# Binding statistics, Newton steps and list pieces behind the y copies on VectorE, and spreading attention's steps up to tile 129

## The chip, the cores and the metric

The kernel runs on one core of a Trainium2 chip. The metric is the device time of one execution in microseconds (us), as the median of several executions. The engines are TensorE (PE, with its weight loads as PEld), VectorE (DVE), ScalarE (ACT), GpSimd (POOL) and SyncE (SP, which here only issues transfers). Transfers that read or write through a list of row numbers (gathers and scatters) are issued by POOL.

## The reference, cut to what matters

8192 tokens of 256 values in 8 sequences of 1024. A layernorm, causal linear attention with 16 heads of 16, and a mixture of 8 experts of which each token uses two; the output is the input plus both.

```python
xn = (x - mean) / sqrt(var + 1e-5)
# attention
q, k = elu(xn @ Wq.T) + 1, elu(xn @ Wk.T) + 1
v = xn @ Wv.T
kv_cumsum = cumsum(k * v over the tokens of a sequence); k_cumsum = cumsum(k)
out = (q . kv_cumsum) / clip(q . k_cumsum, 1e-6, None)
attn = out @ Wo.T
# experts, H = 256, I = 512, E = 8
w, e = top_k(xn @ Wr + br, 2); w = softmax(w)
ffn = sum over the two of w * ((silu(xn @ W1[e]) * (xn @ W3[e])) @ W2[e])
result = x + attn + ffn
```

## The kernel before, in words

**Blocks and attention.** The tokens are worked in 16 blocks of 512 (NBLK), each of 4 chunks of 128 (NCH). Attention is a generator (`block_steps`, L1106) that yields 8 steps for each block and one more at the end, 129 in all (LAST). Below, step b.s is step s of block b. Steps 0 to 2 project q, k and v. Step 3 computes the denominators (den L980; VectorE's over and reciprocal), the scores of chunk 0, and `attend` for the last chunk of the block before. Steps 4 to 7 each take one chunk: `scores` (s_ps L1011, masked by VectorE into s_sb L1018), `carry` (the state of the earlier chunks times q, into o_ps L1030), `weigh` (the scores times v L1048, the new state kv, VectorE's oT L1065 and kv), and `attend` for the chunk before: a_ps L1091 on PE, a copy to at on ACT L1096, and for every second chunk a transfer by POOL (L1099) that adds two chunks of at, one half of a block, to the output in memory. "at(b14 h1)" would be the second half of block 14.

**Expert tiles.** The experts' work is cut into 132 tiles (NM) of 128 rows of one expert. Tiles 0 to 24 (N1 = 25) take tokens of the first four blocks (FB = 4) and are ready at the start; the others take the rest, and their lists of tokens are made while the first tiles run. Some spare tiles follow under a condition. `ffn_step(j)` (L1429) issues: the gathers of later tiles (`ffn_load`, POOL, L1297 and L1302), the weights of tile j + 2 (SP), gate and up for tile j (gu_ps L1391 on PE, silu on ACT L1399, the product hT on VectorE L1402), the second product of tile j - 1 (y_ps L1410 on PE, and its scaled copy y on VectorE, L1417, "the y copy"), and the store of an older tile, a transfer by POOL that adds the rows of y to the output (L1421). What POOL adds to the output, from attention and from tiles, goes in the order in which it is issued.

**Work beside the tiles.** `tile_step(j)` (L1481) is called for each tile. Beside `ffn_step` and attention's steps it holds:

- in tiles 0 to 11, the preparation of block t = 4 + j: the transposes of the normalised block (`turn`, tp L357), its router logits (lg_ps, lg_t), the statistics of a block to come (`stats`, L298: for each of four chunks a bn_stats and a bn_aggr), and for every second block the inverse deviations of two blocks (`deviations`, L307: 17 small VectorE operations, with four Newton iterations for the inverse square root). `normalise(t + 1)` (ACT) needs the deviations, and `turn(t + 1)` in the next tile needs the normalised block;
- in tiles 4, 8 and 12 ("counting" tiles) a part of `route` (L417): VectorE ranks the experts of four blocks, PE counts them (cnt_ps L483), VectorE works the counts into places;
- in tiles 14 to 21, and once in tile 22 (READ = 22), pieces of `second_batch` (L741), a generator that makes the list of the other tiles. `piece(place)` takes its next piece at five places of each tile: ahead of attention's step (0), behind it (1), between the two halves of gate and up (2), behind them (3) and at the tile's end (4). A piece makes two one-hot tables on VectorE (at_place L606 and held L619) and five products on ACT (parts, L624 and L626); the next call multiplies them on PE (held_ps L771), and every fourth of them sums into all_held on VectorE.

**Order.** PE's order is the order of the program text (the tile loop runs under a manual schedule for PE). The other engines are ordered by a scheduler, unless the program binds an instruction behind another: `in_order(...)`, and `tc.issue_after(x)`, under which everything issued goes behind instruction x. Before the change, the routing work of a tile and the statistics and deviations are under `issue_after(last_masked)`, that is behind the latest mask or reciprocal of attention (`last_token` in the first three tiles).

**Buffers of PE's results.** The pool ps_y has two banks, used in turn by y_ps, a_ps, den, lg_ps, lg_t, cnt_ps and held_ps; ps_mm has four, for gu_ps, s_ps and the projections; ps_t has two, for the transposes and o_ps with kv_ps.

**Where attention's steps go.** `attend_upto(upto, put_off=True)` runs steps until `upto` of them are made; most tiles get one step, and where two are due, the second is in some cases left to a later tile or put off behind the gate and up of the same tile. Up to tile 22 the steps are few. From tile 22 on they go by a straight line that reaches the last step at END = NM - 11 = 121: thirteen of these tiles hold two steps, and tiles 122 to 131 none.

Of the kernel before, what the change touches and what calls it, by code (L numbers as in the profile page):

```python
# [51 lines left out]
ALU = mybir.AluOpType  # L52
# [12 lines left out]
def tile_attention_moe(  # L65
# [14 lines left out]
    nc = tc.nc  # L80
# [5 lines left out]
    NCH = TB // P  # L86
    N = B * L
    NBLK = N // TB
# [5 lines left out]
    FB = 4  # L94
# [4 lines left out]
    NM = NF - NR  # L99
# [45 lines left out]
    for t in range(FB):  # L145
        xbs[t] = e_one.tile([P, NCH, H], F32, name=f"xb{t}")
        step = NCH // 2 if t == 0 else NCH
        for c in range(0, NCH, step):
            some = slice(c, c + step)
# [148 lines left out]
    def stats(t, mv):  # L298
        st = f_two.tile([P, NCH, 6], F32, tag="st", name="st")
        for c in range(NCH):  # L300
            nc.vector.bn_stats(st[:, c, :], xbs[t][:, c, :])
            nc.vector.bn_aggr(mv[:, c, :], st[:, c, :])

    def moments_tile(n):
        return f_two.tile([P, n * NCH, 2], F32, tag="mv", name="mv")
# [24 lines left out]
    def normalise(t):  # L330
        xb = xbs.pop(t)
        less, rstd = (tab[:, t * NCH : (t + 1) * NCH, w] for w in (1, 2))
        for c in range(NCH):
            if t < FB and (c % 2 == 0 or t == FB - 1):
                nc.vector.tensor_scalar(
                    xb[:, c, :], xb[:, c, :], rstd[:, c : c + 1], less[:, c : c + 1],
                    ALU.mult, ALU.add,
                )
            else:
                done = nc.scalar.activation(  # L340
                    xb[:, c, :], xb[:, c, :], AF.Identity, bias=less[:, c : c + 1],
                    scale=rstd[:, c : c + 1],
                )
                if t > FB:
                    in_order(done)
        scaled[t] = xb
# [478 lines left out]
    def fetch(t):  # L825
        xnTs[t] = two.tile([P, KC, TB], F32, tag="xnT", name="xnT")
        in_order(
            nc.sync.dma_start(out=xnTs[t].rearrange("p k l -> p (k l)"), in_=xnT_d[t])
        )
# [194 lines left out]
    def carry(t, c):  # L1024

        both_ps = ps_t.tile([P, KC * P + KC * PAIR], F32, tag="t", name="o_ps")
        if t % BLK_PER_SEQ or c:
            o_ps = both_ps[:, 0 : KC * P].rearrange("p (k l) -> p k l", k=KC)
            for hh in range(KC):
                nc.tensor.matmul(  # L1030
                    o_ps[:, hh, :], lhsT=state[0][:, hh, :],
                    rhs=blocks[t][0][:, hh, bass.ts(c, P)],
                    start=(hh == 0), stop=False, skip_group_check=True,
                )
        return both_ps
# [70 lines left out]
    def block_steps(t):  # L1106


        yield from project(t)
        denominators(t)  # L1110
        if t + 1 < NBLK:
            fetch(t + 1)
        waiting = scores(t, 0)
        if behind:
            attend(*behind.pop())
        yield
        done = None
        for c in range(NCH):
            if done:
                attend(*done)  # L1120
            both_ps = carry(t, c)
            coming = scores(t, c + 1) if c + 1 < NCH else None
            oT = weigh(both_ps, *waiting)
            done = t, c, oT
            waiting = coming
            yield
        behind.append(done)
        if t + 1 == NBLK:
            attend(*behind.pop())
            yield  # L1130

    STEPS = 8
    LAST = NBLK * STEPS + 1
# [4 lines left out]
    def attention():  # L1138
        for t in range(NBLK):
            yield from block_steps(t)  # L1140
# [17 lines left out]
    with tc.manual_schedule(engines={EN.DVE, EN.Activation, EN.PE, EN.Pool}):  # L1158
# [85 lines left out]
        mv = moments_tile(1)  # L1244
# [6 lines left out]
    for a in range(4):  # L1251
        some = slice(a * E // 4, (a + 1) * E // 4)
# [35 lines left out]
    ys = {}  # L1288
    entry = {}
# [18 lines left out]
    def ffn_norm(j):  # L1308
        in_order(
            nc.scalar.activation(  # L1310
                xg[j], xg[j], AF.Identity, bias=entry[j][:, 1:2], scale=entry[j][:, 2:3]
            )
        )
# [91 lines left out]
    def ffn_out(j, last=False):  # L1405
        hT = hs.pop(j)
        e = expert_of(j, mybir.EngineType.PE)
        y_ps = ps_y.tile([P, H], F32, tag="y", name="y_ps")
        for i in range(IC):
            done = nc.tensor.matmul(  # L1410
                y_ps, lhsT=hT[:, i, :], rhs=w2_sb[:, bass.ds(e * (IC * H) + i * H, H)],
                start=(i == 0), stop=(i == IC - 1),
            )
            if last:
                in_order(done)
        ys[j] = ffn5.tile([P, H], F32, tag="y", name="y")
        nc.vector.tensor_scalar(ys[j], y_ps, entry.pop(j)[:, 0:1], None, ALU.mult)  # L1417

    def ffn_store(j):
        _, _, _, _, rows, dst_i, i = of_tile(j)  # L1420
# [51 lines left out]
                nc.sync.dma_start(out=wo_sb, in_=woT.rearrange("(k p) o -> p k o", p=P))  # L1472
            )
    LATE = 3
    END = NM - 11
    LISTS = NBLK - FB
    READ = LISTS + 10
    AHEAD = 2 + LISTS // 2 + READ - LISTS
    held = {}

    def tile_step(j):  # L1481
        nonlocal routing
        if j + 1 < TURNED:
            ffn_norm(j + 1)
        if TURNED <= j + 2 < NM:
            ffn_norm(j + 2)
            ffn_halves(j + 2)
        t = FB + j
        turning = 0 < j and t < NBLK
        counting = FB < t <= NBLK and t % ROUND == 0  # L1490

        def piece(place):
            if LISTS + 2 <= j < READ or (j, place) == (READ, 0):
                next(held["lists"])

        def between():
            if turning:
                turn(t)
                if t + 5 < NBLK:
                    load_x(t + 5, nc.scalar)  # L1500
            piece(2)

        def after():
            piece(3)

        def late():
            nonlocal waits
            if waits:
                attend_upto(waits)
                waits = None  # L1510

        def finish():
            if turning:
                held["lgT"] = f_two.tile([P, P], F32, tag="lgT", name="lgT")
                nc.scalar.copy(held["lgT"], logits(t))
            if counting:
                next(routing)
            if t + 1 < NBLK:
                normalise(t + 1)

        if LISTS <= j < LISTS + NBLK - FB:
            rows = slice((t - LISTS) * TB, (t - LISTS + 1) * TB)
            in_order(nc.sync.dma_start(out=out_rows[rows, :], in_=x_rows[rows, :]))
        piece(0)
        if j < LISTS:
            upto = 3 + j // 2
        elif j < READ:
            upto = AHEAD - (READ - j - 1)
        else:
            upto = AHEAD + (LAST - AHEAD) * (j - READ + 1) // (END - READ + 1)  # L1530
        waits = attend_upto(upto, put_off=True)
        if t <= NBLK:
            with tc.issue_after((last_token if j < 3 else last_masked)[0].ins):
                if "lgT" in held:
                    tp = ps_y.tile([P, P], F32, tag="y", name="lg_t")
                    nc.tensor.transpose(tp, held.pop("lgT"), ident)
                    add_logits(t - 1, 1, tp)
                if routing and not counting:
                    for _ in routing:
                        pass  # L1540
                    routing = None
                if counting:
                    routing = route(t - ROUND, t)
                    next(routing)
                of_blocks = [] if j == 0 else [t + 1, t + 2] if j == 1 else [t + 2]
                for a in of_blocks:
                    if a < NBLK:
                        if a % 2 == FB % 2:
                            held["mv"] = moments_tile(2)
                        some = slice(0, NCH) if a % 2 == FB % 2 else slice(NCH, 2 * NCH)  # L1550
                        stats(a, held["mv"][:, some])
                        if a % 2 != FB % 2:
                            deviations(a - 1, 2, held.pop("mv"))
        piece(1)
        ffn_step(j, LATE if N1 < j <= N1 + LATE else 0, between, after, late, finish)
        piece(4)
        if j == LISTS:
            for _ in routing:
                pass
            in_order(  # L1560
                nc.sync.dma_start(
                    out=tab_d[1][1 : 1 + NS * P, :].rearrange("(p i) w -> p (i w)", p=P),
                    in_=tab.rearrange("p i w -> p (i w)"),
                )
            )
            in_order(nc.sync.dma_start(out=tab_d[1][0:1, :], in_=before[0:1, 0:3]))
            held["lists"] = second_batch(taken)
            next(held["lists"])
        if j == N1 + 1:
            copied.append(j)  # L1570
            in_order(nc.sync.dma_start(out=out_rows[0 : FT * P, :], in_=acc_d[:, :]))
# [59 lines left out]
```

## Time and profile before

| quantity | value |
|---|---|
| median of 5 runs | 1278.82 us (1272.17, 1280.89, 1285.35, 1271.82, 1278.82) |
| the profiled execution | 1282.86 us |
| its span, first to last instruction | 1281.2 us |
| mean clock granted to TensorE | 0.982 of full speed |
| busy: PE, DVE, ACT, POOL | 1206.7, 686.2, 588.6, 549.8 us |
| moved by DMA | 252.68 MB, mean 197 GB/s |

The page of the profile shows one execution: busy time of each engine; the span in 40 slices of 32 us, with a digit for the busy tenths of each; the costliest groups of instructions, as line, engine, operation, result and operands, with count, busy time, mean of one, and the idle time of the engine ahead of them with what ended most of it. The timeline shows single instructions or runs of equal ones: start (us from the span's start), duration, engine, line, tiles, and in brackets the idle time ahead and what ended it. The waits list groups of an engine's idle time by the waiting instruction and by what released it: total us, count, longest. Windows give the busy time of each engine within stretches of the span.

### The profile page before, as it was taken

What the parts mean: (1) busy time and instruction counts of PE and PEld (TensorE: products, weight loads), DVE (VectorE), ACT (ScalarE), POOL (GpSimd) and SP (SyncE); (2) the same over time, 40 slices, a digit from 0 to 9 for tenths busy, and PEclk for the clock granted to TensorE, in tenths of its full rate; (3) what the DMA queues carried; (4) which work ended last, traced back from release to release, by engine and by line L of the source; (5) the groups of instructions that cost most, each with busy time, mean ns of one, the idle gap of its engine ahead of it and who ended that gap; (6) DMA issues with size and microseconds to landing.
All of it is one profiled execution on the core that took longest, in us unless ns stands there. A gap on an engine that the chain in (4) does not pass through costs nothing. (4 is left out here: it accounts for less than half of the span.)

```text
span 1281.2 us, 29841 instructions
## 1 busy us (share of the span) xinstructions
PE 1206.7 (94%) x11394; PEld 1056.3 (82%) x11394; DVE 686.2 (54%) x1537; ACT 588.6 (46%) x1098; POOL 549.8 (43%) x474
## 2 busy tenths in 40 slices
PE   8699999899999999999999999999999999999992
PEld 6588887777979888889898989888888888888992
DVE  7676569754444555455554555454535464546320
ACT  5555576592352626262626262626262626262230
POOL 4633343325354544444444444444444444444342
PEclk9899999999999999999999999999999999999996
DMA  9798676558798988988898989898989788978992
GB/s 332 262 276 238 180 220 193 153 162 186 187 224 188 183 212 170 217 168 216 198 198 185 201 183 198 185 201 182 193 193 218 166 215 168 220 164 193 202 234 26
DMA packets 232463, 252.68 MB, mean 197 GB/s; under 512 B 101474, under 2 KB 156386, under 8 KB 232034
## 3 DMA queue, kind: packets, MB, share of 16 engines
q1 hardware_dynamic: 189298, 198.61, 55.0%
q0 software_dynamic: 38272, 43.22, 25.1%
q10 hardware_dynamic: 4752, 8.91, 2.1%
q8 instruction: 94, 1.54, 0.5%
q14 instruction: 47, 0.39, 0.1%
HBM read 187.91 MB, written 44.29 MB: 181 GB/s over the span
## 5 line engine op out<-in xcount | busy, mean ns | idle before, releaser
L1391 PE MATMUL gu_ps<-xgT,w 128*128 128x128 f32 x4224 | 511.3, 279 | 16.7 <-issue 6.1
L1391 PEld LDWEIGHTS gu_ps<-xgT,w 128*128 128x128 f32 x4224 | 495.0, 194 | 35.6 <-issue 17.7
L1421 POOL DMA_INDIRECT out_dram<-y,dst_i x107 | 174.3, 1629 | 273.6 <-DVE y L1417 78.2
L1410 PE MATMUL y_ps<-w_sb,hT 128*128 x1056 | 250.8, 380 | 1.3 <-DVE hT L1402 0.9
L1297 POOL DMA_INDIRECT xg<-in_x_dram,src_i x132 | 135.7, 1028 | 269.4 <-DVE half L1320 155.1
L1399 ACT ACTIVATE hT<-gu_ps 128x512 f32<-128x512 f32 x132 | 79.3, 601 | 315.3 <-PE gu_ps L1391 268.5
L1410 PEld LDWEIGHTS y_ps<-w_sb,hT 128*128 128x128 f32 x1056 | 190.4, 190 | 23.6 <-issue 1.7
L1018 DVE TENSOR_TENSOR s_sb<-s_ps,causal 128x512 f32<-128x512 f32 x256 | 160.2, 680 | 86.3 <-PE s_ps L1011 71.8
L1402 DVE TENSOR_TENSOR hT<-gu_ps,hT 128x512 f32<-128x512 f32 x132 | 90.5, 685 | 67.8 <-PE gu_ps L1391 39.3
L1302 POOL DMA_INDIRECT entry<-tab_d,of_i x107 | 107.7, 1006 | 32.6 <-issue 32.3
L1320 DVE COPY half<-xg 128x512 uint16<-128x512 uint16 x105 | 45.6, 434 | 134.2 <-ACT xg L1310 124.1
L1417 DVE TENSOR_SCALAR y<-y_ps,entry 128x256 f32<-128x256 f32 x132 | 63.6, 482 | 97.0 <-PE y_ps L1410 87.8
L1096 ACT COPY at<-a_ps 128x256 f32<-128x256 f32 x64 | 23.8, 372 | 166.2 <-PE a_ps L1091 166.2
L1310 ACT ACTIVATE xg<-xg,entry 128x256 f32<-128x256 f32 x132 | 78.9, 599 | 7.7 <-DMA entry<-tab_d,of_i 5.3
L1338 ACT COPY xgT<-halfT 128x512 uint16<-128x512 uint16 x105 | 80.1, 763 | 3.3 <-DMA halfT<-half 3.3
L1011 PE MATMUL s_ps<-qm,kT 32*128 32x256 f32 x1024 | 74.8, 403 | 0.0
L1091 PE MATMUL a_ps<-wo_sb,oT 128*128 128x256 f32 x256 | 68.6, 391 | 6.1 <-DVE oT L1065 4.1
L1048 PE MATMUL o_ps<-s_sb,va 128*32 128x128 f32 x2048 | 70.4, 276 | 1.6 <-issue 1.6
L1421 POOL DMA_INDIRECT acc_d<-y,src_i x25 | 43.5, 1741 | 59.8 <-DVE y L1417 25.6
L1048 PEld LDWEIGHTS o_ps<-s_sb,va 128*32 128x32 f32 x2048 | 52.3, 109 | 20.4 <-issue 18.5
L1091 PEld LDWEIGHTS a_ps<-wo_sb,oT 128*128 128x128 f32 x256 | 46.3, 190 | 18.4 <-DVE oT L1065 5.1
L842 PE MATMUL zq<-xnT,wq_sb 128*128 128x512 f32 x128 | 59.0, 603 | 0.0
(236 smaller groups left out, 1399.6 us busy)
## 6 DMA issues: line engine op xcount, KB each, us to landing
w<-in_w_dram SPq DMA_DIRECT2D x264, 512.0 KB
rden<-over SPq DMA_DIRECT2D x128, 64.0 KB
xnT<-xnT_d SPq DMA_DIRECT2D x15, 512.0 KB
out_dram<-at POOLq DMA_DIRECT2D x27, 256.0 KB
out_dram<-in_x_dram SPq DMA_DIRECT2D x12, 512.0 KB
xnT_d<-xnT ACTq DMA_DIRECT2D x11, 512.0 KB
xb<-in_x_dram SPq DMA_DIRECT2D x9, 512.0 KB
w_sb<-in_w_dram SPq DMA_DIRECT2D x4, 1024.0 KB
```

The lines of the kernel that those rows point to most:

```text
L1018: last_masked[0] = nc.vector.tensor_tensor(sm, s_ps[r].rearrange("p k a l -> p (k a) l"), causal_b, ALU.mult)
L1048: nc.tensor.matmul(o_ps[32 * r : 32 * r + 32, hh, :], lhsT=va[:, c, 4 * hh + r, a, :], rhs=s_sb[r][:, 2 * hh + a, :], start=(first and a = ...
L1091: nc.tensor.matmul(a_ps, lhsT=oT[:, hh, :], rhs=wo_sb[:, hh, :], start=(hh == 0), stop=(hh == 1),)
L1297: rows = nc.gpsimd.indirect_dma_start(out=xg[j], out_offset=None, in_=x_rows[:, :], in_offset=bass.IndirectOffsetOnAxis(ap=src_i[:, i : i ...
L1302: nc.gpsimd.indirect_dma_start(out=entry[j], out_offset=None, in_=table[:, :], in_offset=bass.IndirectOffsetOnAxis(ap=num_i[:, i : i + 1], ...
L1310: nc.scalar.activation(xg[j], xg[j], AF.Identity, bias=entry[j][:, 1:2], scale=entry[j][:, 2:3])
L1338: nc.scalar.copy(xgT[j].bitcast(U16).rearrange("p k (l b) -> p b k l", b=2), halves.pop(j).rearrange("p (b k) l -> p b k l", b=2),)
L1391: done = nc.tensor.matmul(ps[:, i, :], lhsT=w13[:, k, bass.ts(i, P)], rhs=xgT[j][:, k, :], start=(k == 0), stop=(k == KC - 1),)
L1399: silu = nc.scalar.activation(hT, gu[0], AF.Silu)
L1402: nc.vector.tensor_tensor(hT, gu[1], hT, ALU.mult)
L1410: done = nc.tensor.matmul(y_ps, lhsT=hT[:, i, :], rhs=w2_sb[:, bass.ds(e * (IC * H) + i * H, H)], start=(i == 0), stop=(i == IC - 1),)
L1421: nc.gpsimd.indirect_dma_start(out=rows[:, :], out_offset=bass.IndirectOffsetOnAxis(ap=dst_i[:, i : i + 1], axis=0), in_=ys.pop(j), in_off ...
```

## The change

Three things are edited.

1. In `block_steps`, a chunk's `carry` is issued ahead of `attend` for the chunk before, on PE, and no longer behind it.
2. `ffn_out` keeps the latest y copy in `held_y`. The list pieces are issued under `issue_after(held_y)`, so that what they issue goes behind the latest y copy on VectorE. The statistics of tile 1 and of the counting tiles, and all deviations, move to `finish()`, which runs behind `ffn_out`, also under `issue_after(held_y)`; the deviations stand there directly ahead of `normalise` in the tile where they are needed, and in tile 1 the statistics of block 6 stay where they were and those of block 7 move. The statistics of the other tiles stay behind the masks.
3. The line along which attention's steps are spread from tile 22 on now ends at tile 129 (NM - 2 is 130, and the 108 tiles from 22 to 129 share the steps) and no longer at 121. Three tiles hold two steps (56, 97 and 129), and tiles 130 and 131 none.

```diff
@@ block_steps
         for c in range(NCH):
+            both_ps = carry(t, c)
             if done:
                 attend(*done)
-            both_ps = carry(t, c)
@@ ffn_out
-        nc.vector.tensor_scalar(ys[j], y_ps, entry.pop(j)[:, 0:1], None, ALU.mult)
+        held_y[0] = nc.vector.tensor_scalar(ys[j], y_ps, entry.pop(j)[:, 0:1], None, ALU.mult)
+
+    held_y = [None]
@@
-    END = NM - 11
...
+    def take_stats(t):
+        second = t % 2 != FB % 2
+        if not second:
+            held["mv"] = moments_tile(2)
+        stats(t, held["mv"][:, second * NCH : (second + 1) * NCH])
@@ piece
-                next(held["lists"])
+                with tc.issue_after(held_y[0].ins):
+                    next(held["lists"])
@@ finish
             if t + 1 < NBLK:
+                if j > 0:
+                    with tc.issue_after(held_y[0].ins):
+                        if t + 2 < NBLK and (counting or j == 1):
+                            take_stats(t + 2)
+                        if t + 2 < NBLK and t % 2 != FB % 2:
+                            deviations(t + 1, 2, held.pop("mv"))
                 normalise(t + 1)
@@ tile_step
-            upto = AHEAD + (LAST - AHEAD) * (j - READ + 1) // (END - READ + 1)
+            upto = min(LAST, AHEAD + (LAST - AHEAD) * (j - READ + 1) // (NM - 2 - READ))
@@ tile_step, under issue_after(last_masked)
-                of_blocks = [] if j == 0 else [t + 1, t + 2] if j == 1 else [t + 2]
-                for a in of_blocks:
-                    if a < NBLK:
-                        if a % 2 == FB % 2:
-                            held["mv"] = moments_tile(2)
-                        some = slice(0, NCH) if a % 2 == FB % 2 else slice(NCH, 2 * NCH)
-                        stats(a, held["mv"][:, some])
-                        if a % 2 != FB % 2:
-                            deviations(a - 1, 2, held.pop("mv"))
+                if t + 2 < NBLK and j > 0 and not counting:
+                    take_stats(t + 1 if j == 1 else t + 2)
```

## The prediction

> **What bounds the kernel now.** I read the page first: busy shares and the slices.
>
> ```profile
> span 1281.2 us, 29841 instructions
> PE 1206.7 (94%) x11394; PEld 1056.3 (82%) x11394; DVE 686.2 (54%) x1537; ACT 588.6 (46%) x1098; POOL 549.8 (43%) x474
> ...
> PE   8699999899999999999999999999999999999992
> ```
>
> TensorE (PE) is busy 94% of the span, so only its 74.5 us of idle time can be won. Next, the windows of 20 us: some 20 us of idle lie before 100, 15 between 100 and 320, 17 between 320 and 1240, and 22.9 after PE's last matmul. The change works on the second and the last. The timeline of the end, whole and for POOL alone, with start and duration:
>
> ```profile
> 1256.31 1.99 PE L1410 MATMUL y_ps<-w_sb,hT 128*128 x8 [0.85 <-DVE hT L1402]
> 1258.34 0.48 DVE L1417 TENSOR_SCALAR y<-y_ps,entry 128x256 f32<-128x256 f32 x1 [2.09 <-PE y_ps L1410]
> ```
>
> ```profile
> 1184.66 1.62 POOL L1421 DMA_INDIRECT out_dram<-y,dst_i  x1 [0.90 <-DVE y L1417]
> ...
> 1190.81 1.32 POOL L1099 DMA_DIRECT2D out_dram<-at  x1 [3.24 <-ACT hT L1399]
> ...
> 1200.19 1.63 POOL L1421 DMA_INDIRECT out_dram<-y,dst_i  x1 [6.68 <-issue]
> ...
> 1264.66 1.55 POOL L1421 DMA_INDIRECT out_dram<-y,dst_i  x1 [2.91 <-issue]
> 1269.27 1.55 POOL L1421 DMA_INDIRECT out_dram<-y,dst_i  x1 [3.05 <-DMA out_dram<-y,dst_i]
> 1273.82 1.55 POOL L1421 DMA_INDIRECT out_dram<-y,dst_i  x1 [3.01 <-issue]
> ```
>
> Each store into the output starts when the one before it has landed. At 1184.66 POOL stores a tile 0.3 us after its y copy; the last y copy ends at 1258.82 and is stored at 1273.82, 15.0 us late. POOL fell behind in the ten tiles without attention (PE spends 5.30 us on each, POOL's stores stand 5.1 to 7.3 us apart there). The third view is the waits of PE between 60 and 320, the fourth the windows behind the longest of them (columns: length, busy time of five engines, granted clock, DMA share, GB/s):
>
> ```profile
> PE cnt_ps L483 <- DVE mv L302: 3.8, 2, 2.0
> PE a_ps L1091 <- DVE oT L1065: 3.6, 2, 2.6
> PE den L980 <- DVE y L1417: 2.0, 2, 1.2
> PE a_ps L1091 <- DVE y L1417: 1.9, 2, 1.0
> ```
>
> ```profile
> 100.60:104.00 3.40, 3.40 (x21) 3.40 (x20) 3.11 (x19) 1.43 (x2) 1.07 (x2) 0.56 0.53 100
> 142.10:145.50 3.40, 3.40 (x18) 3.30 (x17) 2.79 (x18) 1.71 (x2) 1.12 (x2) 0.52 0.43 50
> ```
>
> PE waits for VectorE's (DVE's) counts and y copies, and after each of the two waits for cnt_ps it also runs at half clock for 3.4 us.
>
> **The spreading, on PE.** 111 steps fall on 108 tiles instead of 100: three tiles hold two steps instead of thirteen, and two tiles at the end none instead of ten. No instruction is added. Tiles without attention show no PE idle, and a step's own waits go with it, so PE's end stays: 0, between -3 and +3 (the six waits of gu_ps for ACT's at copy, 4.7 us in all, may lengthen or vanish by some half). Carry ahead of attend swaps 0.61 us and 1.03 us of matmuls: 0, but for one place counted below.
>
> **The spreading, at the end.** Steps 127 and 128 move from tile 121 to tile 129. I lay the end of the new order on the old trace: steps 125 to 128 with their tiles look as at 1174 to 1197, where gu_ps of the last attention tile starts (1196.99). From gu_ps of tile 129 to the last matmul PE took 1239.39 to 1258.30, 18.9 us; so PE would end at 1215.9 on this scale. All gathers are issued by then. POOL's order is store 126, at, store 127, at, then stores 128 to 131. Distances from start to start: store to at 4.65 (1157.84 to 1162.49) or 6.15 (1184.66 to 1190.81); at to store 6.36 (1162.49 to 1168.85) or 9.38 (1190.81 to 1200.19); store to store 4.55 at the end. Store 126 starts at 1184.66. Taking the middle for the first pair, where the weights of the old trace load as well, and the short ones behind, where gathers and then weights have ended: 1184.66 + 5.40 + 7.87 + 4.65 + 6.36 + 4.65 + 4.55 + 4.55 = 1222.7 for store 131; its y is ready at 1216.4. From the last store's start to the end the old trace took 7.4: 1230.1, or 14.2 us after PE instead of 22.9. Gain 8.7. With every short row it is 11.3; with every long row (and 5.38, 1254.82 to 1260.20, for the last three) -0.4.
>
> **Statistics and Newton steps.** The instructions stay, their place on DVE changes. Gains: in the counting tiles the route's chain is no longer cut by statistics, so the waits for cnt_ps go: 1.76 + 2.01 + 0.26, and with them the half clock (gu_ps 3.39 and 2.94 us instead of 1.95: 2.4), and one lg_t wait of 0.59: 7.1. Loss: in tile 1 the y copy can start at 68.8, and behind it now stand, in the new order, the statistics of block 7 and then block 6's Newton steps, mixed with the mask s_sb of tile 2 and with statistics of blocks 8 and 9. From start to start in this stretch a statistics pair takes 0.41, a small step among others 0.1, a mask 0.61: 0.40 for the copy, 1.55 for block 7, 1.95 for over, its reciprocal and the first small steps, 2.85 for four masks with a step each, 3.65 for ten Newton steps, six and a half statistics pairs and lg_all: the deviations are ready at 79.2. ACT then normalises block 6 (2.08), and PE, whose transposes of it ran at 74.74, can go on with gu_ps at 82.0 instead of 75.61: 6.4 lost, and one more half clock, 1.4. Behind it in queue on ACT stand only xg and the copies for the same tile. In tile 4, fifteen Newton steps of 0.20 stand ahead of the first mask, and gu_ps waits for the bank that it frees, then the transposes for ACT: 1.6. Tiles 6, 8 and 10 have attend and carry between (1.6 us more of matmuls), which hide it; without that cover they would cost 1.6 each. Sum 7.1 - 9.4 = -2.3. Bounds: +1.5 (tile 2 costs 5.0 and tile 4 0.6) and -7.8 (the small steps at their whole duration of 0.17, tile 4 2.2, and no clock won back).
>
> The Trainium skill, TensorE: Matmul & The Clock Gate, Part 1, says that the clock halves after at least one idle window of about 3.4 us. The row differs: 0.56 follows a wait of only 1.76. By the page 2.4 of the gain would not be there, and the whole would come to 5.4 instead of 7.8.
>
> **List pieces (tiles 14 to 22).** The y copy now follows hT directly. PE's waits for it at den, at_ps and twice a_ps (1.19, 0.97, 0.97, 0.96: 4.1) go, since held_ps and y hold both y banks there. What is late next is the first piece of each tile, behind the copy: copy, all_held, at_place, held 2.2, then ACT's parts 1.4 behind the at copy: 3.95 after y_ps, while PE needs it after attention's step, at 4.3. Hidden by 0.35. In tile 17 three held in a row stand ahead of the masks, and the last needs parts that ACT finishes late: gu_ps waits 1.4 for its bank, and carry, now first, waits 0.9 for kv; in tile 18 0.4. Sum 4.1 - 2.7 = +1.4; bounds +4.1 and -9.5 (1.7, the third held behind parts at 5.35 plus a mask against 4.85, in eight tiles, 13.6).
>
> **Sum.** 8.7 - 2.3 + 1.4 = 7.8. The profiled execution took 1282.9 (span 1281.2 and 1.7 around it), 4.0 above the median of the five runs; taken off that median, 1278.8, it gives 1271.0.
>
> **Rivals.** Slower: VectorE's pieces become the bound. If in all eight list tiles held stands ahead of the masks as in tile 17, PE loses 1.7 and, through the half clock, 1.4 in each, 24.8; the sum is 8.7 - 2.3 + 4.1 - 24.8 = -14.3: 1293.1. It passes 1% from 2.9 us a tile. For it: DVE was busy 17.84 of 20 us from 200 to 220. Against: in most tiles of the new order a mask comes before the third held.
> The end doesn't clear: at in the queue costs 9.4 twice, POOL stays as late as before, gain 0 there: -0.9, 1279.7. For it: the row at 1190.81. Against: no gathers stand between any more.
> Faster: the short rows hold at the end (11.3), the stall of tile 2 is small (+1.5) and lists win their 4.1: 16.9, 1261.9. For it: unloaded stores stand 4.55 apart. Against: the Newton steps are behind the copy in the order itself.
>
> **How the numbers follow.** Forecast 1271.0: 0.50, own range 1264 to 1277. The end doesn't clear 0.13, slower rival 0.14, faster rival 0.23. 1% is 12.8 us, about what a measurement of this kernel can tell from no change (its five runs span 13.5). A small part of the forecast (0.02) lies below 1266: faster 0.25, same 0.61, slower 0.14. The range, 1261 to 1285, takes in all but the slower rival.
>
> **What would show it.** Right: PE's last matmul 11 to 17 us before the span's end, and stores at the end 4.6 apart; no wait for cnt_ps; one wait of tp (L357) near 76, some 5 to 6 us, on ACT's xb; no wait of a_ps or den for y between 195 and 260. Wrong: a tail of 20 us or more; gu_ps waiting for s_sb in every list tile; PE's busy time at the start as before.

## The result, and the profile after

The changed kernel takes 1282.84 us (median of 37 runs, 1274.41 to 1288.40), the kernel before, over all its runs, 1278.37 us (63 runs). The ratio is 1.0036, with a 95% interval from 1.0025 to 1.0048: by the ratio 4.6 us longer, where 7.8 us shorter were forecast. The profiled execution took 1286.1 us, 3.3 above the median, much as that of before (1282.86, 4.5 above).

From the page of the changed kernel:

```profile
span 1284.4 us, 29801 instructions
PE 1210.7 (94%) x11394; PEld 1051.3 (82%) x11394; DVE 687.6 (54%) x1537; ACT 588.1 (46%) x1098; POOL 550.4 (43%) x474
...
PE   8689998898999999999999999999999999999994
```

The last slice went from 2 tenths to 4, so the tail became shorter; the third, seventh and tenth slice (64 to 96, 193 to 225 and 289 to 321 us) read 8 where 9 stood. The end, from the timeline of all engines (POOL's stores and PE's last matmuls):

```profile
1242.42 1.27 POOL L1099 DMA_DIRECT2D out_dram<-at  x1 [3.35 <-issue]
1250.74 1.64 POOL L1423 DMA_INDIRECT out_dram<-y,dst_i  x1 [7.05 <-issue]
1256.64 1.28 POOL L1099 DMA_DIRECT2D out_dram<-at  x1 [4.26 <-DMA out_dram<-y,dst_i]
1261.94 1.63 POOL L1423 DMA_INDIRECT out_dram<-y,dst_i  x1 [4.02 <-DMA out_dram<-at]
...
1266.49 1.99 PE L1410 MATMUL y_ps<-w_sb,hT 128*128 x8 [0.85 <-DVE hT L1402]
...
1277.15 1.56 POOL L1423 DMA_INDIRECT out_dram<-y,dst_i  x1 [3.03 <-DMA out_dram<-y,dst_i]
```

PE ends at 1268.5 and the span 15.9 us later, instead of 22.9. But PE itself ends 10.2 us later than before (1258.3). The waits of PE between 175 and 336 us, over the list tiles, show most of the reason (total us, times, longest):

```profile
PE held_ps L771 <- ACT parts L626: 7.1, 6, 4.1
PE o_ps L1030 <- DVE kv L1077: 2.2, 1, 2.2
PE o_ps L1030 <- DVE kv L1068: 1.4, 1, 1.4
PE held_ps L771 <- DVE at_place L606: 1.3, 1, 1.3
PE held_ps L771 <- DVE kn L812: 1.2, 1, 1.2
...
PE den L980 <- DVE y L1417: 0.2, 1, 0.2
```

The same view of the kernel before has

```profile
PE held_ps L771 <- ACT parts L626: 1.7, 2, 1.5
```

The waits for y are gone, as the change has it (0.2 instead of 4.1), and the products of the lists now wait for parts that ACT makes (7.1 instead of 1.7).

To see where time goes in kernels whose steps lie in other tiles, I take four marks from PE's timeline: the start of y_ps for tiles 0, 12, 25 and 131. Between tile 12 and 25 lie the list tiles; the steps differ between the kernels only from tile 31 on. The tail runs from the end of the last matmul to the end of the span.

| traced execution | 0 to 12 | 12 to 25 | 25 to 131 | tail |
|---|---|---|---|---|
| before | 120.1 | 146.7 | 922.6 | 22.9 |
| changed | 122.3 | 155.2 | 920.8 | 15.9 |
| difference | +2.2 | +8.5 | -1.8 | -7.0 |

With 1.3 us that the changed kernel's trace was later at the first mark, these add up to 3.2, the difference of the spans. The list tiles cost more than the tail brought. These are single executions, and some of what they show (a half clock behind a wait, the length of the tail) differs between executions of the same code, as the experiments show; 1 to 2 us in one column say little.

### The profile page after: what moved, and what is told of

The parts are those of the page before. It is cut to its first block, busy times and chain, and to the rows that moved or that the text cites. A ratio compares the mean times of both kernels' runs of the same rounds, so it can differ in the third digit from the quotient of the medians.

```text
span 1284.4 us, 29801 instructions
## 1 busy us (share of the span) xinstructions
PE 1210.7 (94%) x11394; PEld 1051.3 (82%) x11394; DVE 687.6 (54%) x1537; ACT 588.1 (46%) x1098; POOL 550.4 (43%) x474
## 4 chain that ended last, share of the span: by engine, by line
PE 84%; DVE 6%; ACT 3%; DMA 3%; issue 2%; another core or an unknown queue 1%; SPq 0%; POOL 0%; POOLq 0%; ACTq 0%; DVEq 0%
PE gu_ps L1391 36%; PE y_ps L1410 17%; PE s_ps L1011 5%; PE o_ps L1048 5%; PE a_ps L1091 4%; PE zkk L863 4%; PE zkv L863 4%; PE zq L842 4%; PE o_ps L1030 2%; PE tp L357 1%; DVE s_sb L1018 1%; PE held_ps L771 1%; PE den L980 1%; PE o_ps L1058 1%
## 5 line engine op out<-in xcount | busy, mean ns | idle before, releaser
L1402 DVE TENSOR_TENSOR hT<-gu_ps,hT 128x512 f32<-128x512 f32 x132 | 90.6, 686 | 79.2 <-PE gu_ps L1391 47.2
L1048 PEld LDWEIGHTS o_ps<-s_sb,va 128*32 128x32 f32 x2048 | 52.8, 111 | 21.6 <-issue 21.5
L1011 PEld LDWEIGHTS s_ps<-qm,kT 32*128 32x128 f32 x1024 | 47.6, 186 | 23.0 <-issue 17.7
L1099 POOL DMA_DIRECT2D out_dram<-at x27 | 36.0, 1332 | 53.8 <-DMA out_dram<-y,dst_i 34.5
```

The source lines that it names most:

```text
L1011: nc.tensor.matmul(s_ps[r][:, hh].rearrange("p a l -> p (a l)"), lhsT=kT[rows, hh, span], rhs=qm[rows, hh, :, span], start=True, stop=True,)
L1048: nc.tensor.matmul(o_ps[32 * r : 32 * r + 32, hh, :], lhsT=va[:, c, 4 * hh + r, a, :], rhs=s_sb[r][:, 2 * hh + a, :], start=(first and a = ...
L1402: nc.vector.tensor_tensor(hT, gu[1], hT, ALU.mult)
```

## The experiments

They ran in four sets, each beside runs of the kernel before. Each set ran on a chip of its own. That kernel took 1275.51 us in the first set and 1247.22, 1247.43 and 1248.41 in the others; so ratios are always against before in the same set, and the marks of the first set are not set against those of the others. The chip of the result above is not on record; its traces look like those of the first set.

### First set: one part at a time

**Spreading alone.** The list pieces, statistics and carry stay as before.

```diff
-            upto = AHEAD + (LAST - AHEAD) * (j - READ + 1) // (END - READ + 1)
+            upto = min(LAST, AHEAD + (LAST - AHEAD) * (j - READ + 1) // (NM - 2 - READ))
```

> Only the third edit: attention's steps spread up to tile 129, the rest as before. Theory A (the tail and the list tiles carry the result): the tail after PE's last matmul shrinks from 22.9 to about 16 us, as in the changed kernel's profile (15.9), and PE's end stays: 1271.5 us, ratio 0.9945. Rival B (the spreading itself costs PE in the middle of the kernel, at the tiles that now hold a step, what it brings at the end): 1278 to 1282 us, with the same short tail but PE's last matmul 7 to 10 us later than before.

**List pieces alone.**

```diff
-                next(held["lists"])
+                with tc.issue_after(held_y[0].ins):
+                    next(held["lists"])
```

> Only the list pieces are bound behind the y copy; carry, statistics and spreading as before. Theory A: the loss of the changed kernel arises in tiles 14 to 22, where PE's lag grew from 3.5 us (tile 12) to 13 us (tile 22): 1286 to 1289 us, ratio 1.007, with PE waiting some 7 us in held_ps for ACT's parts, above all in tiles 20 and 21, which hold projection steps. Rival C (the waits of o_ps for kv, 2.2 and 1.4 us, come with carry ahead of attend, and the pieces alone take away 4.1 us of waits for y): 1275 to 1279 us.

**Statistics and Newton steps alone.** The edits of `finish` and of `tile_step` behind `issue_after(last_masked)`, as in the change.

> Only the statistics and the Newton steps are bound behind the y copy. Theory A: as the step of the prediction has it, a loss of about 2.3 us (tile 2 loses 6, the waits for cnt_ps go): 1280.7 us, ratio 1.002. Rival D (the stall of tiles 2 to 4, where the lag went to 10.2 us, is worth more than what the counting tiles give back): 1284 us or more. Rival E (it is a gain by itself, since only the profiled execution lost 1.5 us ahead of it): 1276 us.

**Carry ahead of attend alone.**

```diff
+            both_ps = carry(t, c)
             if done:
                 attend(*done)
-            both_ps = carry(t, c)
```

> Only carry is issued ahead of attend. Theory A: it swaps 0.61 and 1.03 us of matmuls, no difference: 1278.4 us, within 1 us. Rival C (carry waits for the new state kv, which VectorE makes late where it is full, and attend no longer covers that wait): 1281 us or more, with waits of o_ps for kv in the profile.

| kernel | ratio | 95% interval | 0 to 12 | 12 to 25 | 25 to 131 | tail |
|---|---|---|---|---|---|---|
| spreading alone | 0.9914 | 0.9885 to 0.9943 | 116.5 | 145.6 | 920.0 | 11.0 |
| lists alone | 1.0053 | 1.0030 to 1.0076 | 116.5 | 151.0 | 919.5 | 22.9 |
| statistics alone | 1.0029 | 1.0009 to 1.0049 | 122.1 | 145.8 | 918.6 | 23.1 |
| carry alone | 1.0020 | 1.0000 to 1.0041 | 119.2 | 146.6 | 920.6 | 21.5 |

The spreading, the pieces and the statistics each move their own column. The spreading costs PE nothing from 25 to 131 (920.0, where the three others, with the old line, have 918.6 to 920.6), so rival B falls, and it shortens the tail, by more than theory A had (11.0 instead of 16). The pieces lengthen the list tiles to 151.0, where the three kernels with free pieces have 145.6 to 146.6, with 6.5 us of waiting for ACT's parts; rival C falls. The statistics lengthen the first tiles: 122.1 against 116.5 to 119.2 here, and the ratio agrees with theory A (3.7 us); rival E falls, and rival D (1284 us or more, a ratio from 1.0044) lies at the interval's end. Carry alone shows nothing in the first three columns that the others don't; its 2.6 us by the ratio are at the edge of what can be told from none (the interval begins at 1.0000). The waits of its rival C are there, 3.5 and 1.4 us of o_ps for kv, but they stand where a_ps waited 3.6 for oT and 0.9 more for y.

The first column varies by itself, since the clock does. Before the change and with carry alone, PE runs gu_ps at half clock behind both waits for cnt_ps (3.39 and 2.94 us, 3.47 and 2.81); with the spreading alone and the lists alone it takes 1.95 each time, though the instructions there are the same and the waits alike (1.76 and 2.01 with the spreading, as before; 1.43 and 2.01 with the lists). That is most of the step from 116.5 to 119.2 and 120.1.

The end with the spreading alone, POOL's timeline:

```profile
1224.94 1.27 POOL L1099 DMA_DIRECT2D out_dram<-at  x1 [2.59 <-issue]
1231.84 1.64 POOL L1421 DMA_INDIRECT out_dram<-y,dst_i  x1 [5.63 <-DVE oT L1065]
1236.31 1.28 POOL L1099 DMA_DIRECT2D out_dram<-at  x1 [2.82 <-ACT xgT L1338]
1241.02 1.63 POOL L1421 DMA_INDIRECT out_dram<-y,dst_i  x1 [3.43 <-DMA out_dram<-at]
...
1255.58 1.56 POOL L1421 DMA_INDIRECT out_dram<-y,dst_i  x1 [2.96 <-DMA out_dram<-y,dst_i]
```

The same instructions in the same order as in the changed kernel, from the first at to the last store in 30.6 us instead of 34.7: at to store 6.9 instead of 8.3, store to at 4.5 instead of 5.9, and the last four stores 14.6 instead of 15.2 apart. Over the twelve traces in which the line ends at 129, the tail was 11.0 to 16.0 us, and in eight of them between 15.5 and 16.0; one kernel, run in the second and in the fourth set, has 11.8 and 15.5.

### Second set: the parts taken out of the changed kernel

**Without list binding.** The changed kernel with `next(held["lists"])` as before.

> The changed kernel with the list pieces left as before: carry, statistics and spreading remain. Theory A (the parts add up, and the pieces are what turned a gain into a loss): the spreading alone gave a ratio of 0.991, the statistics 1.003, carry 1.002, together 0.996, some 1273 us where before has 1278; the tail after PE's last matmul 11 to 16 us; waits of held_ps for ACT's parts back at 1.7 us. Rival F (the gain of the spreading needs attend ahead of carry: its tail was 10.9 us alone and 15.9 in the changed kernel): 1.000 or more, with a tail of 16 us.

**Pieces bound in the chunk tiles only**, and **statistics without tile 1's** (before, with the statistics and Newton steps bound behind y from tile 2 on; those of tile 1 stay under `issue_after(last_token)`), both edits shown against the changed kernel:

```diff
-                with tc.issue_after(held_y[0].ins):
-                    next(held["lists"])
+                if 14 < j < 20:
+                    with tc.issue_after(held_y[0].ins):
+                        next(held["lists"])
+                else:
+                    next(held["lists"])
```

> The changed kernel, but the pieces are bound behind the y copy only in tiles 15 to 19, which hold the denominators or a chunk, and not in tiles 14, 20, 21 and 22, which hold projections. Theory A (the loss sits in the projection tiles, where parts stand behind the exponentials on ACT): some 6 to 10 us below the changed kernel, 0.994 to 0.997 of before. Rival G (the loss sits in the chunk tiles, where the three pieces stand ahead of masks and kv, as the prediction's slower rival has it): 1.002 of before or more.

```diff
-                if j > 0:
+                if j > 1:
                     with tc.issue_after(held_y[0].ins):
-                        if t + 2 < NBLK and (counting or j == 1):
+                        if t + 2 < NBLK and counting:
                             take_stats(t + 2)
...
-                if t + 2 < NBLK and j > 0 and not counting:
-                    take_stats(t + 1 if j == 1 else t + 2)
+                if j == 1:
+                    take_stats(t + 1)
+                    take_stats(t + 2)
+                    deviations(t + 1, 2, held.pop("mv"))
+                elif t + 2 < NBLK and j > 0 and not counting:
+                    take_stats(t + 2)
```

> Only the statistics and Newton steps, and those of tile 1 (statistics of blocks 6 and 7, Newton steps of block 6) stay as before; the rest is bound behind the y copy. Theory A (the step of the prediction: tile 1's chain costs 7.8, what is left gains 7.1 less 1.6 for tile 4): 5 us below before, ratio 0.996. Rival H (what the counting tiles give back depends on the lag that tile 2 made, so that without it nothing is won): ratio 1.000 or above.

**Spreading with these statistics**, no carry, no list binding:

> The spreading and the statistics without tile 1's, no carry and no list binding. Theory A (parts add): 0.991 times 0.996, ratio 0.987, some 1261 us where before has 1278. Rival: the two share the same wait or the same half clock, and it stays at 0.991.

| kernel | ratio | 95% interval | 0 to 12 | 12 to 25 | 25 to 131 | tail |
|---|---|---|---|---|---|---|
| without list binding | 0.9945 | 0.9927 to 0.9963 | 123.3 | 141.6 | 900.3 | 11.8 |
| bound in tiles 15 to 19 | 0.9960 | 0.9945 to 0.9975 | 122.0 | 143.3 | 899.1 | 12.6 |
| statistics without tile 1's | 0.9971 | 0.9957 to 0.9986 | 117.1 | 142.6 | 899.6 | 21.8 |
| spreading with these | 0.9888 | 0.9867 to 0.9909 | 119.8 | 142.5 | 900.6 | 15.6 |

Without the list binding the change is a gain, with carry ahead of attend and a tail of 11.8, so rival F falls. With the pieces bound in the denominators' and chunks' tiles it stays one (rival G falls; the two intervals overlap). The statistics without tile 1's are a gain (rival H falls), 3.6 us of the 5 expected, and the last kernel beats both kernels of this case.

### Third set: where the lists lose

**Pieces bound in the projection tiles only** (`if j < 15 or 19 < j`, the rest of the change as it is):

> The changed kernel with the pieces bound behind the y copy only in tiles 14, 20, 21 and 22, which hold projections; in tiles 15 to 19 they are left as before. Theory A (the loss of the list binding sits in the projection tiles): as the changed kernel, ratio 1.001 to 1.004. Rival G (it needs the chunk tiles too): 0.996 or below.

**The change without carry's move:**

> The changed kernel with attend ahead of carry again, as before. Theory A (carry by itself is no more than the 0.2% that it cost alone): 1.000 to 1.003. Rival C (with the pieces bound, masks and kv are late, and attend no longer covers carry's wait for kv, 2.2 and 1.4 us in the changed kernel's trace): 0.998 or below, and these waits of o_ps for kv gone.

**Parts on VectorE.** The whole change, but in tiles 14, 20 and 21 the five products of a piece are VectorE's:

```diff
+        if parts_on_dve[0]:
+            nc.vector.tensor_scalar(parts[:, :, 0, :], held, row128[:, 0:1], None, ALU.mult)
+            for i in range(PART):
+                nc.vector.tensor_scalar(
+                    parts[:, i, 1, :], held[:, i, :], float(1 + j * NT + a + i), None, ALU.mult
+                )
+            return at, parts
...
+                parts_on_dve[0] = j in (14, 20, 21)
```

> The changed kernel, but in tiles 14, 20 and 21 the pieces' parts are made by VectorE and not by ACT. Theory A (held_ps waits because parts stand behind the projection's exponentials and masked queries in ACT's queue, 4.15 us at once in tile 21): these waits for ACT go, PE's lag over tiles 13 to 25 shrinks by 4 to 7 us, ratio 0.997 to 0.999. Rival I (a piece behind the y copy is late whatever engine makes its parts, since at_place and held themselves come late and VectorE's five more operations come on top): the same lag, 1.003 or more, with held_ps waiting for VectorE.

**The line to tile 127:**

```diff
-            ... // (NM - 2 - READ))
+            ... // (127 - READ + 1))
```

> The spreading and the statistics without tile 1's, with the line of attention's steps ending at tile 127 and not at 129. Theory A (the tail is POOL's queue of stores behind the last at; PE takes 5.30 us for a tile without attention and POOL 4.6 for a store once the gathers are out, so two more such tiles let POOL catch up): a tail of 9 to 11 us after PE's last matmul, 2 to 4 us below the version that ends at 129, ratio 0.985 to 0.987. Rival J (POOL falls behind from the first tile without attention, as it did with ten of them): a tail of 16 us or more, ratio 0.990 or above.

| kernel | ratio | 95% interval | 0 to 12 | 12 to 25 | 25 to 131 | tail |
|---|---|---|---|---|---|---|
| bound in 14 and 20 to 22 | 1.0007 | 0.9994 to 1.0019 | 122.8 | 150.2 | 899.2 | 14.0 |
| change without carry | 0.9995 | 0.9977 to 1.0014 | 121.8 | 148.6 | 900.5 | 15.8 |
| parts on VectorE | 0.9963 | 0.9949 to 0.9977 | 121.9 | 143.0 | 900.0 | 15.6 |
| line to 127 | 0.9933 | 0.9914 to 0.9952 | 119.4 | 142.7 | 898.8 | 14.7 |

The loss is in the projection tiles (150.2 with these alone; rival G falls), and it is ACT: with the parts taken off it in these tiles, the list tiles take 143.0, as with free pieces (142.7 on the same chip), and rival I falls. Tile 21 in the changed kernel, one line of DVE and ACT's timeline, with PE's two lines of the same stretch behind it:

```profile
284.30 0.61 DVE L619 TENSOR_TENSOR held<-rows,in_row 128x440 bf16<-128x440 f32 x1
285.18 1.06 ACT L809 ACTIVATE neg<-zq 128x512 f32<-128x512 f32 x2
286.26 1.28 ACT L810 ACT_TABLE_LOAD   x1
287.56 1.15 ACT L810 ACTIVATE neg<-neg 128x512 f32<-128x512 f32 x2
288.61 0.65 ACT L624 ACTIVATE parts<-held,row 128x440 bf16<-128x440 bf16 x1
289.16 2.54 ACT L852 ACTIVATE qm<-qT,par 128x512 f32<-128x512 f32 x4
291.61 0.83 ACT L626 ACTIVATE parts<-held 128x110 bf16<-128x110 bf16 x4
291.94 0.90 PE L771 MATMUL held_ps<-parts,at_place 128*128 128x220 bf16 x4 [4.15 <-ACT parts L626]
292.63 3.72 PE L1391 MATMUL gu_ps<-xgT,w 128*128 128x128 f32 x16
```

and the same place before the change:

```profile
272.82 0.66 ACT L624 ACTIVATE parts<-held,row 128x440 bf16<-128x440 bf16 x1
273.37 0.84 ACT L626 ACTIVATE parts<-held 128x110 bf16<-128x110 bf16 x4
274.11 0.66 ACT L624 ACTIVATE parts<-held,row 128x440 bf16<-128x440 bf16 x1
274.66 0.84 ACT L626 ACTIVATE parts<-held 128x110 bf16<-128x110 bf16 x4
275.40 0.58 ACT L809 ACTIVATE neg<-zq 128x512 f32<-128x512 f32 x1
```

Before, the parts of two pieces that PE needs in this tile stand on ACT ahead of the projection's elu (the negative part L809, its exponential L810 with a table load, the masked queries L852). Now the first piece is still in time (its parts end at 285.27, and held_ps runs at 285.45 without a wait), but VectorE makes the second held 2.5 us behind the y copy (281.82 to 284.30), its parts miss that place and go behind the elu, and the last four of them even behind qm. PE waits 4.15 us, and runs at half clock afterwards (windows; granted clock is the third number from the end):

```profile
285.83:291.90 6.07, 1.96 (x18) 1.79 (x17) 2.07 (x4) 6.04 (x11) 0.00 (x0) 0.82 0.58 183
292.60:296.10 3.50, 3.50 (x18) 3.48 (x17) 1.09 (x2) 3.47 (x9) 0.00 (x0) 0.50 0.02 5
```

In tile 20 it is 1.16 of waiting (put down to VectorE's kn, which itself waited 1.55 for ACT's neg) and 0.45 for ACT's parts, and a gu_ps at half clock, 3.47 instead of 1.96. With the parts on VectorE the waits of held_ps for parts between 172 and 345 us are:

```profile
PE held_ps L780 <- DVE parts L629: 2.1, 1, 2.1
PE held_ps L780 <- ACT parts L635: 1.8, 3, 1.1
```

The 2.1 us lie in tile 14, where VectorE is now the later one.

With the pieces bound, the list tiles take 148.6 without carry's move and 152.5 with it in the fourth set, 151.0 and 155.2 in the first traces (lists alone, changed). Nearly all of both differences lies in two tiles. In tile 17, from one y_ps to the next, PE takes 13.1 and 13.2 us without the move and 15.5 twice with it. In the fourth set's changed kernel and without carry's move:

```profile
224.80 0.68 PE L1030 MATMUL o_ps<-qT,kv 128*128 128x128 f32 x4 [2.23 <-DVE kv L1077]
220.83 1.13 PE L1091 MATMUL a_ps<-wo_sb,oT 128*128 128x256 f32 x4 [1.29 <-DVE oT L1065]
```

Where kv is late, attend no longer lies ahead of carry; the wait is longer, and s_ps behind it runs at half clock. In tile 20, which holds no carry, the same two kernels wait alike (1.16 or 1.17, and 0.44 or 0.45), but the clock falls in one only:

```profile
266.77 3.55 PE L1391 MATMUL gu_ps<-xgT,w 128*128 128x128 f32 x16
261.38 2.02 PE L1391 MATMUL gu_ps<-xgT,w 128*128 128x128 f32 x16
```

With the pieces bound in the projection tiles only, carry moved, this gu_ps takes 2.02 too. So some 2.4 us of the difference are the move's, and 1.6 are not. The ratio without the move, 0.9995, is between the two theories and decides nothing. The line to 127 was expected to let POOL catch up; the tail is 14.7, within the spread of the others, and the time by the ratio is above that of 129, so rival J is nearer, though its 16 us were not reached.

### Fourth set: the parts on one chip, one after the other

The changed kernel, then without list binding, then also without carry, then also without tile 1's statistics and Newton steps.

> The changed kernel itself, beside the three versions below on one chip. Theory A (list pieces in the projection tiles cost 8 to 9 us, carry some 2, tile 1's chain some 7 of which the counting tiles give 5 back, the spreading gains 9 to 11): 1.002 to 1.004 of before.

> The changed kernel with the list pieces left as before, on the same chip as the changed kernel. Theory A: 0.007 to 0.009 below it. Rival K (the 0.9% between the two came from two different chips): less than 0.004 below it.

> The spreading and the statistics with tile 1's, without carry and list binding. Theory A: against the version with carry it shows carry's own cost, 0.001 to 0.003. Rival (carry costs nothing, the 0.2% measured alone was chance): equal within 0.001.

> The spreading and the statistics without tile 1's, on the same chip. Theory A: 0.005 to 0.007 below the version with tile 1's chain (stall of 7 us at the transposes of block 6 in tile 2): 0.987 to 0.989 of before.

| kernel | ratio | 95% interval | 0 to 12 | 12 to 25 | 25 to 131 | tail |
|---|---|---|---|---|---|---|
| changed | 1.0006 | 0.9992 to 1.0021 | 122.0 | 152.5 | 900.3 | 16.0 |
| no list binding | 0.9953 | 0.9935 to 0.9970 | 122.0 | 143.5 | 899.5 | 15.5 |
| also no carry | 0.9939 | 0.9920 to 0.9958 | 121.9 | 142.7 | 900.1 | 15.8 |
| also no tile 1 chain | 0.9908 | 0.9889 to 0.9928 | 120.6 | 142.6 | 900.4 | 16.0 |

The list binding costs 0.0053 (6.6 us by the times, 9.0 by the marks; the traced execution of the changed kernel is the longest of its twelve, 1254.01 us, so its marks may say too much), carry 0.0014, which is within its uncertainty, tile 1's chain 0.0031, hardly more than its own. The first lies between the 0.007 of theory A and rival K's 0.004, and its uncertainty, some 0.0023 by the two intervals, reaches both. On this chip the whole change can't be told from before; in the result above it is 4.6 us slower.

Taking tile 1's chain out gave back less than the 0.005 to 0.007 expected. In the last kernel, timelines of DVE and PE in tile 2:

```profile
62.16 0.17 DVE L328 SCALAR_TENSOR_TENSOR tab<-mv,tab 128x8 f32<-128x8 f32 x1
62.24 0.48 DVE L1417 TENSOR_SCALAR y<-y_ps,entry 128x256 f32<-128x256 f32 x1
62.78 0.64 PE L980 MATMUL den<-ksum,own_of 128*32 128x128 f32 x16 [3.65 <-DVE y L1417]
```

The chain now stands ahead of the y copy again, and den waits 3.65 for it, where the trace of before had 0.81: here PE starts tile 0's y_ps some 10 us earlier (57 instead of 67), and VectorE ends the chain only 7.4 earlier (the first line stands at 69.53 before). Behind the wait s_ps and gu_ps run at half clock (2.09 and 3.78 instead of 1.15 and 2.05).

## Why the prediction was wrong

Between the two traced executions the span grew by 3.2 us where the sum had 7.8 less, 11.0 apart. Of these, 9.9 lie in the list tiles, where +1.4 was forecast and 8.5 were lost.

**The end: right.** A tail of 14.2 us was forecast, 15.9 came in the changed kernel, 11.0 to 16.0 in all; the gain of 8.7 was 7.0 here. From the first at to the last store POOL took 34.7 us, where the sum had 32.6: the store to the second at 5.9 instead of 4.65, the last three distances 15.2 together instead of 13.8, and the two from at to store 8.3 and 5.3 instead of 7.87 and 6.36, which nearly cancel.

**The spreading on PE: right.** 0 was forecast; from 25 to 131 the new line takes 920.0 and 920.8 in the traces of the result and of the first set, where the old one takes 918.6 to 922.6, and 899.1 to 900.6 on the other chips, where the old one takes 899.6. (Of the idle time that the prediction started from, the part between 320 and 1240 us is 15.8, not 17; nothing rests on it.)

**Statistics and Newton steps: right in place, and in size within the uncertainty.** A net loss of 2.3 was forecast. The trace has 2.2, the chip 3.7 alone (1.1 to 6.2). That the trace agrees to 0.1 is luck: the 2.4 us of half clock that the gain counted are in this trace of before and in that of carry alone, and not in the two others of the first set with the same instructions, against which the loss would be 5.8. Tile 2, step by step, in the changed kernel's timeline:

```profile
70.08 0.48 DVE L1417 TENSOR_SCALAR y<-y_ps,entry 128x256 f32<-128x256 f32 x1 [1.19 <-PE y_ps L1410]
79.80 0.14 DVE L328 SCALAR_TENSOR_TENSOR tab<-mv,tab 128x8 f32<-128x8 f32 x1
79.97 2.07 ACT L340 ACTIVATE xb<-xb,tab 128x256 f32<-128x256 f32 x4 [1.07 <-DMA rden<-over]
80.63 0.33 PE L357 MATMUL tp<-ident,xb 128*128 128x128 f32 x1 [2.36 <-ACT xb L340]
83.22 2.78 PE L1391 MATMUL gu_ps<-xgT,w 128*128 128x128 f32 x16
```

The copy starts at 70.08, 1.3 later than 68.8 on the scale of before; on that scale the deviations are ready at 78.6 (forecast 79.2) and gu_ps goes on at 81.9 (forecast 82.0). The wait itself looks shorter than forecast (2.36, not 5 to 6), because gu_ps ahead of it had waited 1.98 for its bank and ran at half clock (3.68). The waits for cnt_ps on mv are gone, as forecast; one of 0.59 for y came in their place.

**List pieces: wrong, and this turned the sign.** The step that failed is "What is late next is the first piece of each tile", with "Hidden by 0.35", and so the sum 4.1 - 2.7 = +1.4. The 4.1 came. But the 3.95 of the step counts ACT's parts "behind the at copy", which only tiles with attend have, and the loss of 2.7 is worked out on tiles 17 and 18; the tiles with projections, 14, 20 and 21, have no term of their own. There ACT's order was left out: the first piece is hidden in tile 21, but the second, made late by the same binding, misses its place ahead of the elu, PE waits 4.15 us for it and then runs at half clock. All waits for ACT's parts came to 7.1 us instead of 1.7. Alone, the binding costs some 5 us by the marks (151.0 against 145.6 to 146.6), and inside the change 6.6 by the times; with it off, or with the parts off ACT in these three tiles, the change is a gain (0.9953 and 0.9963). The lower bound, -9.5, was about as large but rested on another mechanism, masks behind held in the chunk tiles; the run with the pieces bound only there shows 0.0015 of loss, within the intervals. The slower rival had that mechanism too, so it is not what happened.

**Carry: 0 was forecast, and alone it may be so** (1.0000 to 1.0041). The single wait for kv that was counted, 0.9, measured 2.23, with the half clock behind it (s_ps took 2.09 instead of 1.15). By the marks of tile 17 the two moves together cost 2.4 more than the binding alone, and the sum added them as if they were independent; the times can't confirm it, since the versions with and without the move ran on different chips (1.0006 and 1.0036 against 0.9995).

**What is left open:** why the tail was 11 to 12.6 us in three traces and 14 to 16 in the others; from the first at to the second POOL takes 11.4 to 11.9 us in the three and 13.2 to 14.4 in the others, and what sets this was not tried. Open too is why the clock falls behind a wait in one execution and not in the next.

## What to carry to other kernels

When work is bound later on one engine, go through every tile kind that it lands in, and on each follow its results to the engine that takes them: there they lose their place in a queue whose next entry may be long, and one delay of 2.5 us became a wait of 4.15. A stall costs more where the clock falls behind it, but with waits of 1.4 to 2 us it fell in some executions of this kernel and not in others: give such a term a chance, and look at a second trace before it is counted whole. And measure parts of a bundle one by one: here the spreading and most of the statistics were worth 1% together, and a third part hid it.

## What the runs showed of the hardware

- The clock fell to half after short waits of PE, and did not always. Behind the two waits for cnt_ps (1.43 to 2.01 us) it fell before the change and with carry alone, and with the spreading alone and the lists alone it did not, with the same instructions. Behind 1.16 and 0.45 in tile 20 it fell in two traces and not in three (gu_ps 3.47 and 3.55, and 2.02). Behind 1.98 us in tile 2 it fell; with the statistics alone, behind 1.91 in the same place, not directly (gu_ps 2.05). Behind 4.15 us in tile 21 it fell in all five traces that have this wait (gu_ps 3.31 to 3.72). The Trainium skill, TensorE: Matmul & The Clock Gate, Part 1, asks for an idle window of about 3.4 us; the row with 4.15 us of waiting (clock 0.50 after it) agrees, those with 1.61 and 1.98 do not.
- One chip needs 2.2% more than three others for the same kernel. From tile 25 to 131 PE needs 919 to 921 us on the one and 899 to 901 on the others, at a granted clock of 1.00 between 400 and 1000 us; in that stretch PE is idle 9.3 of 600 us with the statistics alone (first set) and 0.5 with the statistics without tile 1's (second set), two kernels with the same order there. Why was not looked into.
- VectorE makes the parts of a piece in 0.33 and 0.48 us where ACT takes 0.65 and 0.83.
